# A two-layer kernel: layer 0 put in program order, its gated blocks cut finer, and blocks combined earlier

## The chip, the cores and the metric

One core of one Trainium2 chip runs the whole program in one launch. The metric is device microseconds of that core per execution, as the median of several runs; the profiled execution is a single one. The kernel before has a median of 1210.88 us over 9 runs (1198.3 to 1218.23).

## The reference, cut to what matters

The input x is 16 x 256 tokens of 128 numbers. Each of two layers computes `x + s * silu(g)`, where s comes from a mixing branch and g from a mixture of experts, both of them over the same layer norm of x.

```python
# layer 0
xn = layernorm(x)
q, k, v = xn@Wq, xn@Wk, xn@Wv                 # 4 heads of 128 (q, k) and 32 (v)
gk = log_sigmoid(xn@Wgk1@Wgk2 + bgk2) / 16    # decays
S_t = diag(exp(gk_t)) S_{t-1} + k_t^T v_t     # gated recurrence, per head
o_t = DK**-0.5 * q_t S_t
s = (rmsnorm(o) * gnw * silu(xn@Wg)) @ Wo
comb = top-2 of softmax(xn @ Wg0.T), normed to 1      # 8 experts
h = xn @ W1[e].T + b1[e]; a, b = split(h)
g = sum_e comb[e] * ((a * sigmoid(b)) @ Wo0.T + bo)
x = x + s * silu(g)
# layer 1
xn = layernorm(x)
s = causal_attention(xn, 16 heads of 8) @ w_proj
# top-2 of 16 experts: tanh(xn@mag) * cos(softplus(xn@freq) + 0.1 + phase), times down
x = x + s * silu(rmsnorm(g) * norm_w)
```

## The kernel before, in words

**Tiling.** The 4096 tokens are eight blocks of 512 (`BT`), four tiles of 128 tokens each (`NTL`). A block spans two sequences. All eight blocks stay in SBUF: `xs` holds x, `xns` its norm, `xnTs` the transposed norm; the mixing result `s_sbs[b]` is written over `xnTs[b]`.

**Norms** (`layernorm_T`, L203; `norms`, L653). DVE takes mean and variance (L207, L208), POOL raises to the power -1/2 (L200, L201), DVE scales (L213), PE transposes (L216), ACT copies (L217). Eight matmuls (L448) give a block's scores for the eight experts.

**Routing** (`route`, L237; the same function serves both layers). It picks two experts a token, writes the normed rows with their two weights to DRAM (`xnd`, L276), ranks the tokens by expert and makes lists: `toks` (which rows a tile of 128 slots takes), `rows` (where its results go), `emap` (the expert of each tile). Layer 0 has 71 such tiles, layer 1 has 79. The lists come out of one-hot products on DVE, ACT and PE (L333 to L347) in 16 steps. In all `route` has 25 steps (its yields).

**Gated blocks.** `decays(b)` (L455) computes the decays by ACT (Abs, Exp, Ln, L473 to L475), a running sum by a DVE scan (L478), the two scalings (L485, L488), then q and k scaled by them (L501, L503), `kg`, v and the gate `sg`. Its PSUM tiles of two banks (`pz`, `pq`) come from the pool `p2` with two buffers. `mixed(b)` (L535) multiplies k and q (L544), masks (L545), multiplies by v (L555, L562), norms (L571 to L578) and projects into `s_sbs[b]` (L582). `gated` (L658) interleaves `decays(b)` with `mixed(b - 1)`.

**Layer-0 experts** (`experts0`, L586) go through the 71 tiles in 18 batches of four (the last of three). For a batch POOL fetches the rows by an indirect DMA for each tile (`slot_in`, L368), SP loads the weights of each tile's expert (L601, L603), PE transposes the rows (L608), multiplies (L618), ACT and DVE gate two tiles at a time (L625 to L633), PE multiplies again (L642), DVE adds the bias and weighs (L646, L648), and POOL scatters the results to `yd` (`slot_out`, L380). The fetches of a batch wait for the v copy of a gated block (`vcopies`, with the constants `FIRST` and `SPAN`).

**Order in layer 0.** Norms, routing, experts and gated blocks are emitted interleaved (L670 to L688), and a scheduler of the compiler then places each engine's instructions by its own estimates. Four copies of the layer-1 expert weights from DRAM to DRAM (`late`, L185 to L189, 2 + 2 + 1 + 1 MB) wait for the v copies of the fourth and fifth gated blocks (L689).

**Layer 1** stands under `manual_schedule`: ACT, PE, DVE and SP run in program order, written out by hand. `combined(b)` (L950) loads both results of a block from `yd` (L394; each load waits for every scatter of layer 0), makes the new x, its norm and transpose, and the layer-1 scores. `attention` (L737) yields small pieces, 254 of them with work; `fill(n)` (L1159) emits n pieces and before each of them one POOL instruction, a fetch and a scatter by turns, ordered behind the DVE instruction last marked by `passed`. The combines take `fill(4)` at each of their last eight steps, `route` takes one piece at each of its 25 steps, a batch of eight experts takes about 20, and what is left runs beside `finished(b)`, which ends a block.

Of the kernel before, what the change touches and what calls it, by code (L numbers as in the profile page):

```python
# [10 lines left out]
F32 = mybir.dt.float32  # L11
# [7 lines left out]
P = 128  # L19
# [20 lines left out]
FIRST = 2  # L40
SPAN = 5
PACE = 1
# [18 lines left out]
def two_layer_kernel(  # L61
# [77 lines left out]
    mhalf = cst.tile([P, 16], F32, name="mhalf")  # L139
    nc.gpsimd.memset(mhalf, -0.5)  # L140
# [43 lines left out]
    late = []  # L184
    late.append(nc.sync.dma_start(bank[:, :, 0:H1], freq))  # L185
    late.append(nc.sync.dma_start(bank[:, :, H1 : 2 * H1], mag))
    for c in range(H1 // P):
        cs = slice(2 * H1 + c * D, 2 * H1 + (c + 1) * D)
        late.append(nc.sync.dma_start(bank[:, :, cs], down[:, c * P : (c + 1) * P, :]))  # L189
# [9 lines left out]
    def rsqrt_(out_, var, mul, eps):  # L199
        nc.gpsimd.tensor_scalar(out_, var, mul, eps, ALU.mult, ALU.add)  # L200
        nc.gpsimd.tensor_tensor(out_, out_, mhalf[:, : out_.free_size()], ALU.pow)  # L201

    def layernorm_T(pool, ps, xb, xnT, xn):  # L203
        mv = pool.tile([P, NTL, 2], F32, tag="mv", name="mv")
        for t in range(NTL):
            st = pool.tile([P, 6], F32, tag="st", name="st")
            nc.vector.bn_stats(st, xb[:, t, :])  # L207
            nc.vector.bn_aggr(mv[:, t, :], st)  # L208
        rs = pool.tile([P, NTL], F32, tag="rs", name="rs")
        rsqrt_(rs, mv[:, :, 1], 1.0, 1e-5)  # L210
        pt = ps.tile([P, NTL, P], F32, tag="ps", name="pt")
        for t in range(NTL):
            nc.vector.tensor_scalar(  # L213
                xn[:, t, :], xb[:, t, :], mv[:, t, 0:1], rs[:, t : t + 1], ALU.subtract, ALU.mult
            )
            nc.tensor.transpose(pt[:, t, :], xn[:, t, :], ident)  # L216
        nc.scalar.copy(xnT, pt.rearrange("p t k -> p (t k)"))  # L217
# [19 lines left out]
    def route(pool, ps, sc, ne, slt, lay, emap, rm, tag="ps"):  # L237
# [49 lines left out]
        pc = ps.tile([P, ne], F32, tag=tag, name="pc")  # L287
# [13 lines left out]
        rk = ps.tile([P, ne, NT32], F32, tag=tag, name="rk")  # L301
# [25 lines left out]
        pT = ps.tile([P, 2, slt], F32, tag=tag, name="pT")  # L327
# [60 lines left out]

    def results(pool, lay, b, tag="gg"):
# [35 lines left out]
    nc.gpsimd.dma_start(sb_nw, normw.partition_broadcast(P))  # L425
    with ExitStack() as cg:
        big = cg.enter_context(tc.tile_pool(name="gbig", bufs=2, side="right"))
        wk_ = cg.enter_context(tc.tile_pool(name="gwk", bufs=2, side="right"))
        hp = cg.enter_context(tc.tile_pool(name="ghp", bufs=2, side="right"))
        rt = cg.enter_context(tc.tile_pool(name="grt", bufs=1, side="right"))  # L430
        p2 = cg.enter_context(tc.tile_pool(name="gp2", bufs=2, space=PSUM))
        ps = cg.enter_context(tc.tile_pool(name="gps", bufs=3, space=PSUM))
# [7 lines left out]
        nc.scalar.preload_act_table_set(LN_EXP)  # L440
        held, vcopies = {}, []
        sc0 = rt.tile([P, NT32, E0], F32, name="sc0")
        rm0 = starts(rt, E0)

        def scores(b, w, out_, ne, bias=None):
            pl = ps.tile([P, NTL, ne], F32, tag="ps", name="plg")
            for t in range(NTL):
                nc.tensor.matmul(pl[:, t, :], xnTs[b][:, t * P : (t + 1) * P], w, start=True, stop=True)  # L448
            o = out_[:, b * NTL : (b + 1) * NTL, :]
            if bias is None:  # L450
                nc.scalar.copy(o, pl)
            else:
                nc.vector.tensor_tensor(o, pl, bc(bias.unsqueeze(1), [P, NTL, ne]), ALU.add)

        def decays(b):  # L455
# [6 lines left out]
            nc.scalar.activation(lowT, p_low, AF.Identity, bias=one16)  # L462
            eg = big.tile([P, GH, BT], F32, tag="eg", name="eg", bufs=1)
            eis = []
            mid = wk_.tile([P, GH * NTL], F32, tag="mid", name="mid")
            for u in range(GH // 2):
                hs = slice(2 * u, 2 * u + 2)
# [4 lines left out]
                sp = wk_.tile([P, 2, BT], F32, tag="sp", name="sp", bufs=1)  # L472
                nc.scalar.activation(sp, pz, AF.Abs)  # L473
                nc.scalar.activation(sp, sp, AF.Exp, scale=-1.0)
                nc.scalar.activation(sp, sp, AF.Ln, bias=1.0)  # L475
                nc.vector.scalar_tensor_tensor(sp, pz, 0.0, sp, ALU.min, ALU.subtract)
                cum = wk_.tile([P, 2, BT], F32, tag="cum", name="cum", bufs=1)
# [6 lines left out]
                nc.vector.tensor_tensor(ev, ev, ib(mid[:, 2 * u * NTL : (2 * u + 2) * NTL], CH), ALU.subtract)  # L484
                nc.scalar.activation(eg[:, hs], cum, AF.Exp, scale=1.0 / 16.0)  # L485
                ei = wk_.tile([P, 2, BT], F32, tag="ei", name="ei")
                eis.append(ei)
                nc.scalar.activation(ei, cum, AF.Exp, scale=-1.0 / 16.0)  # L488
                yield
# [3 lines left out]
            for u in range(GH // 2):  # L493
                hs = slice(2 * u, 2 * u + 2)
                for dst_, w_ in ((qg, sb_wq), (kk, sb_wk)):
                    pq = p2.tile([P, 2, BT], F32, tag="p2", name="pq")
                    for c in range(2):
                        h = 2 * u + c
                        nc.tensor.matmul(pq[:, c], w_[:, h * DK : (h + 1) * DK], xnT, start=True, stop=True)
                    if dst_ is qg:  # L500
# [169 lines left out]
        for _ in norms(0):  # L670
            pass
# [590 lines left out]
```

## Time and profile before

| | us |
|---|---|
| median of 9 runs (1198.3 to 1218.23) | 1210.88 |
| the profiled execution | 1219.11 |
| its span, first to last instruction | 1217.4 |
| PE busy | 892.7 (73%) |
| DVE busy | 759.3 (62%) |
| ACT busy | 562.3 (46%) |
| POOL busy | 401.6 (33%) |

PE holds the matmuls, PEld the weight loads that overlap them, DVE the vector engine, ACT the scalar engine, POOL GpSimd, SP the queue that issues most DMAs. The costliest lines of layer 0 on PE are L618 (78.6 us busy), L642 (53.3), L544 (41.4), the two uses of L499 (34.2 and 32.7) and L608 (22.3, with 52.5 us of idle time before it). The mean granted clock of TensorE is 0.847. Sums over the whole span hide that its stages have different limits, so the stages are read one by one.

### The profile page before, as it was taken

What the parts mean: (1) busy time and instruction counts of PE and PEld (TensorE: products, weight loads), DVE (VectorE), ACT (ScalarE), POOL (GpSimd) and SP (SyncE); (2) the same over time, 40 slices, a digit from 0 to 9 for tenths busy, and PEclk for the clock granted to TensorE, in tenths of its full rate; (3) what the DMA queues carried; (4) which work ended last, traced back from release to release, by engine and by line L of the source; (5) the groups of instructions that cost most, each with busy time, mean ns of one, the idle gap of its engine ahead of it and who ended that gap; (6) DMA issues with size and microseconds to landing.
All of it is one profiled execution on the core that took longest, in us unless ns stands there. A gap on an engine that the chain in (4) does not pass through costs nothing. (4 is left out here: it accounts for less than half of the span.)

```text
span 1217.4 us, 17549 instructions
## 1 busy us (share of the span) xinstructions
PE 892.7 (73%) x6394; PEld 628.1 (52%) x6394; DVE 759.3 (62%) x1442; ACT 562.3 (46%) x973; POOL 401.6 (33%) x439
## 2 busy tenths in 40 slices
PE   5858895758798775388656559887888888887762
PEld 3535564545576664244333336565566656665531
DVE  5699673616465522666764636875776688578464
ACT  2335564535466343332211226554555565556283
POOL 4100344323545354001200053472464446343310
PEclk9879897979899887557867769898899899889775
DMA  4060129272333231310040043143134313330231
GB/s 115 1 114 1 35 80 210 76 122 73 87 90 95 77 106 43 91 49 4 13 59 1 0 148 116 34 135 116 43 121 131 124 39 126 122 82 31 68 104 52
DMA packets 88413, 95.40 MB, mean 78 GB/s; under 512 B 22228, under 2 KB 64040, under 8 KB 88328
## 3 DMA queue, kind: packets, MB, share of 16 engines
q1 hardware_dynamic: 78632, 74.32, 22.7%
q0 software_dynamic: 9696, 19.97, 6.4%
q8 instruction: 50, 0.82, 0.3%
q14 instruction: 35, 0.29, 0.1%
HBM read 78.03 MB, written 22.51 MB: 83 GB/s over the span
## 5 line engine op out<-in xcount | busy, mean ns | idle before, releaser
L380 POOL DMA_INDIRECT yd<-og,row x150 | 155.4, 1036 | 265.8 <-DVE og L648 141.0
L832 POOL TENSOR_SCALAR_AFFINE_SELECT pr<-pr 128x1024 f32<-128x1024 f32 x64 | 70.9, 1111 | 318.2 <-ACT pr L829 317.9
L368 POOL DMA_INDIRECT xg<-xnd,tok x150 | 149.1, 994 | 77.5 <-issue 34.7
L822 PE MATMUL Sk<-qm,kT 32*128 32x256 f32 x768 | 129.2, 461 | 42.2 <-ACT pr L829 29.4
L793 PE MATMUL Sq<-km,qT 32*128 32x256 f32 x768 | 132.0, 462 | 11.7 <-DVE negm L803 6.6
L829 ACT ACTIVATE pr<-Sk 128x1024 f32<-128x1024 f32 x96 | 97.4, 1016 | 72.4 <-PE Sk L822 70.9
L803 DVE TENSOR_REDUCE negm<-Sq 128x8 f32<-128x1024 f32 x64 | 78.1, 1220 | 44.6 <-PE Sk L822 26.3
L822 PEld LDWEIGHTS Sk<-qm,kT 32*128 32x128 f32 x768 | 77.1, 216 | 55.4 <-ACT pr L829 37.7
L793 PEld LDWEIGHTS Sq<-km,qT 32*128 32x128 f32 x768 | 73.1, 214 | 61.6 <-issue 37.5
L633 DVE SCALAR_TENSOR_TENSOR gt<-pf,nb,sg 128x128 f32<-128x128 f32 x142 | 40.1, 344 | 81.2 <-ACT sg L629 81.2
L618 PEld LDWEIGHTS pf<-xgT,wt 128*128 128x128 f32 x568 | 73.9, 208 | 12.7 <-issue 6.3
L618 PE MATMUL pf<-xgT,wt 128*128 128x128 f32 x568 | 78.6, 294 | 2.5 <-DVE kk L503 1.3
L625 ACT ACTIVATE sg<-pf,nb 128x128 f32<-128x128 f32 x142 | 40.8, 367 | 59.9 <-PE pf L618 55.3
L642 PE MATMUL pe<-sb_wo,gt 128*128 128x128 f32 x284 | 53.3, 318 | 18.0 <-DVE gt L633 17.5
L642 PEld LDWEIGHTS pe<-sb_wo,gt 128*128 128x128 f32 x284 | 46.3, 221 | 32.4 <-DVE gt L633 22.6
L608 PE MATMUL pxt<-ident,xg 128*128 128x128 f32 x71 | 22.3, 354 | 52.5 <-DMA xg<-xnd,tok 52.4
L1074 PE MATMUL pe<-wt,th 128*128 128x128 f32 x316 | 48.8, 318 | 8.3 <-DVE th L1065 8.3
L787 PE MATMUL Sq<-mq,identb 128*128 128x512 bf16 x128 | 44.1, 430 | 14.7 <-DVE mx L801 7.0
L801 DVE TENSOR_REDUCE mx<-Sq 128x8 f32<-128x1024 f32 x32 | 39.0, 1219 | 24.4 <-PE Sk L822 13.7
L1074 PEld LDWEIGHTS pe<-wt,th 128*128 128x128 f32 x316 | 45.2, 228 | 15.7 <-issue 10.1
L1026 ACT ACTIVATE z<-pf 128x512 f32<-128x512 f32 (+1 forms) x40 | 23.7, 593 | 52.3 <-PE pf L1022 52.3
L1034 DVE SCALAR_TENSOR_TENSOR vt<-z,wt 128x256 f32<-128x256 f32 x79 | 45.8, 620 | 1.4
(278 smaller groups left out, 2046.3 us busy)
## 6 DMA issues: line engine op xcount, KB each, us to landing
wt<-bank SPq DMA_DIRECT2D x79, 385.0 KB
wt<-in_w_dram SPq DMA_DIRECT2D x71, 256.0 KB
gg<-yd SPq DMA_DIRECT2D x32, 256.0 KB
xnd<-xnx SPq DMA_DIRECT2D x16, 260.0 KB
xg<-xnd,tok POOLq DMA_INDIRECT x150, 2.9
yd<-og,row POOLq DMA_INDIRECT x150, 3.9
x<-in_x_dram SPq DMA_DIRECT2D x8, 256.0 KB
bank<-in_freq_dram SPq DMA_DIRECT2D x1, 2048.0 KB
```

The costliest lines, as they stand in the source:

```text
L368: return nc.gpsimd.indirect_dma_start(out=xg[:, i, :], out_offset=None, in_=xnds[lay], in_offset=bass.IndirectOffsetOnAxis(ap=toks[lay][:, ...
L380: give = nc.gpsimd.indirect_dma_start(out=yds[lay], out_offset=bass.IndirectOffsetOnAxis(ap=rows[lay][:, j : j + 1], axis=0), in_=og[:, i, ...
L618: nc.tensor.matmul(pf[:, i, c, :], wts[i0 + i][:, c * P : (c + 1) * P], xgT[:, i0 + i, :], start=True, stop=True,)
L642: last = nc.tensor.matmul(pe[:, i, :], gts[i // 2][:, i % 2, c, :], sb_wo0[:, c, :], start=(c == 0), stop=(c == 1))
L787: nc.tensor.matmul(S[:, c], identb, mq, start=True, stop=False, skip_group_check=True)
L793: nc.tensor.matmul(S[:, c, js, :], qT[part][r, tq], km[r, js, tk], start=not diag, stop=True, skip_group_check=True,)
L803: passed(nc.vector.tensor_reduce(ng, S, AX.X, ALU.max, negate=True))
L822: nc.tensor.matmul(S[:, c, js, :], kT[part][r, tk], qm[r, js, :], start=True, stop=True, skip_group_check=True,)
L829: nc.scalar.activation(pr, S, AF.Exp, scale=scale)
L832: pooled(nc.gpsimd.affine_select(pr_, pr_, pattern=[[0, 8], [1, P]], compare_op=ALU.is_ge, fill=0.0, base=0, channel_multiplier=-1,))
L1034: nc.vector.scalar_tensor_tensor(v[:, ks, :], z[:, ks, :], INV2PI, ib(wts[i0 + i][:, WROW - 2 :], P), ALU.mult, ALU.add)
L1074: nc.tensor.matmul(pe[:, i - i0, :], ths[i // 2][:, 2 * (i % 2) + c, :], wts[i][:, 2 * H1 + c * D : 2 * H1 + (c + 1) * D], start=(c == 0), ...
```

## The change

Layer 0 now also stands under `manual_schedule`: ACT, PE, DVE and SP follow the program's text, with this driver in place of the interleaving at L670 to L690:

```diff
         main = gated()
-        for _ in main:
...
+        with tc.manual_schedule(engines={ET.Activation, ET.PE, ET.DVE, ET.SP}):
+            nc.scalar.preload_act_table_set(LN_EXP)
+            with tc.tile_pool(name="gpn", bufs=2, space=PSUM) as pn, tc.tile_pool(name="grt", bufs=1, side="left") as rt:
...
+                for _ in normed0(0, pn):
+                    pass
+                copies = bank_copies()
+                first = itertools.chain(
+                    staged(normed0(b, pn) for b in range(1, NB)),
+                    route(rt, pn, sc0, E0, SLT0, 0, emap0, rm0, "n", {"tag": "nT", "bufs": 1}),
+                )
+                for i, _ in enumerate(first):
+                    if i % 2:
+                        next(main)
+                    if i >= 12:
+                        next(copies, None)
...
+            due = 0.0
+            for _ in experts0(hp, pe_):
+                spread()
+                due += 1.0 / RATE
+                while due >= 1.0:
+                    due -= 1.0
+                    next(main, None)
...
+            with tc.tile_pool(name="gpc", bufs=2, space=PSUM) as pc_:
+                c_ps[:] = [pc_, "pc"]
+                cstream = staged([combined(b) for b in range(NB)], lambda b: b in mixed_)
+                for _ in main:
+                    next(cstream, None)
```

`bank_copies` yields the four DRAM copies one after the other, on SP's queue, without a wait. `staged` (moved up from layer 1) starts one generator a step and advances all that have started. `RATE` is 0.85. Counted from the text: the norms take 10 steps and route 25, with 17 gated pieces beside them; the experts take 109 steps with 128 pieces; 31 pieces are left for the last loop, and at its start six blocks are mixed.

**Norms.** `normed_T` serves both layers; ACT takes Ln and Exp where POOL took a power:

```diff
-        rsqrt_(rs, mv[:, :, 1], 1.0, 1e-5)
+        nc.scalar.activation(rs, mv[:, :, 1], AF.Ln, bias=eps5)
+        nc.scalar.activation(rs, rs, AF.Exp, scale=-0.5)
+        yield
```

**Gated blocks.** `decays` has ten pieces and `mixed` twelve (seven and four before). The parts of `decays` become functions and are emitted like this; the arithmetic is the same:

```diff
-        p2 = cg.enter_context(tc.tile_pool(name="gp2", bufs=2, space=PSUM))
-        ps = cg.enter_context(tc.tile_pool(name="gps", bufs=3, space=PSUM))
+        p2 = cg.enter_context(tc.tile_pool(name="gp2", bufs=1, space=PSUM))
+        ps = cg.enter_context(tc.tile_pool(name="gps", bufs=2, space=PSUM))
...
+            logs(0)
+            yield
+            sums(0)
+            logs(1)
+            yield
+            scales(0)
+            yield
+            sums(1)
+            scaled(0, qg, sb_wq)
+            yield
+            scales(1)
+            scaled(0, kk, sb_wk)
+            yield
+            scaled(1, qg, sb_wq)
+            yield
+            scaled(1, kk, sb_wk)
+            yield
```

`logs` holds the pz matmuls and the three ACT instructions, `sums` the DVE instructions up to the subtraction (L476 to L484), `scales` the two Exp, `scaled` a pq and its DVE instruction. The tiles `sp` and `cum` get a second buffer.

**Experts.** They have PSUM of their own (`pf` two banks, one bank `pe` for the transposes and the second product), go tile by tile, and ask for the rows and weights of the next batch at the start of a batch. `wanted` and `given` are the lists of fetches and scatters still to be issued:

```diff
+            for k, (j0, n) in enumerate(batches):
+                xg, wts, nbs = got
+                if k + 1 < len(batches):
+                    got = loads(*batches[k + 1])
+                gts, pend = [], []
+                for i in range(n):
+                    pf = pe_.tile([P, 4, P], F32, tag="pf", name="pf0", bufs=2)
...
+                    for f in pend:
+                        f()
...
+                    pend = [gate]
+                    gts.append(gt)
+                    yield
+                for f in pend:
+                    f()
+                if k + 1 < len(batches):
+                    while any(args[1] == 0 for args in wanted):
+                        fetch(1)
+                    xgT = turned(got[0], batches[k + 1][1])
+                yield
+                pe = pe_.tile([P, CP0, D], F32, tag="pe", name="pe0", bufs=1)
...
+                given.extend((og, 0, j0 + i, i) for i in range(n))
+                yield
+            give(len(given))
```

`gate` of a tile (the two DVE instructions of L633) is emitted one step late. `turned` holds the transposes and the xgT copy. `loads` puts a batch's rows on `wanted` and issues its weight loads on SP (six weight buffers, five before; three row buffers, two before).

**The POOL queue.** `fetch`, `give`, `behind`, `pooled` and `passed` are moved from layer 1 to where both layers reach them; the body of `fill`'s turn-taking becomes

```diff
+    def spread():
+
+        turn[:] = [not turn[0]]
+        if wanted and (turn[0] or not given):
+            fetch(1)
+        else:
+            give(1)
```

Each fetch and scatter waits for the DVE instruction marked last (`behind`), and keeps the program's order on POOL (`pooled`). In layer 0 one `spread` goes with each of the experts' steps: six for a batch of four. Many DVE instructions of `decays`, `mixed` and the experts are now marked.

**Combines.** `combined` moves to layer 0 with its text as it was (its tiles get two buffers throughout, `gg` among them); what is left of it after the last gated piece runs with three attention pieces a step:

```diff
-                for i, _ in enumerate(staged([combined(b) for b in range(NB)])):
-                    if i >= 4:
-                        fill(4)
...
+            for _ in cstream:
+                fill(3)
```

By count the first seven blocks are combined in the loop over the last gated pieces, and four steps are left for the eighth. Route 1 and the layer-1 experts take their attention pieces as before, 25 and 169; layer 1 else differs only in the side of SBUF on which some pools lie.

## The prediction

> **What bounds the kernel now.** I read the stages first: busy time of each engine in stretches cut where the trace shows a stage begin or end (columns: stretch, then PE, PEld, DVE, ACT, POOL busy us with instructions, granted clock, DMA share, GB/s).
>
> ```profile
> 13.40:66.60 53.20, 41.39 (x132) 26.03 (x132) 36.06 (x110) 18.93 (x33) 9.64 (x13) 0.88 0.11 25
> 66.60:121.60 55.00, 40.44 (x257) 27.13 (x258) 51.78 (x87) 26.96 (x37) 1.50 (x8) 0.84 0.39 64
> 121.60:160.00 38.40, 33.08 (x227) 21.95 (x226) 25.62 (x53) 24.86 (x39) 10.17 (x12) 0.91 0.17 42
> 160.00:300.00 140.00, 101.99 (x668) 74.47 (x668) 69.13 (x119) 71.40 (x139) 51.03 (x48) 0.89 0.51 114
> 300.00:440.00 140.00, 117.88 (x791) 89.57 (x790) 74.72 (x139) 75.78 (x151) 66.10 (x64) 0.90 0.33 92
> 440.00:487.00 47.00, 27.00 (x158) 24.02 (x156) 12.46 (x36) 14.93 (x38) 21.28 (x24) 0.79 0.24 62
> 487.00:590.00 103.00, 70.27 (x380) 42.93 (x380) 69.42 (x173) 33.92 (x61) 6.24 (x6) 0.67 0.15 43
> 590.00:703.00 113.00, 58.76 (x396) 33.98 (x394) 71.57 (x112) 20.60 (x26) 12.90 (x18) 0.73 0.13 22
> 703.00:1145.00 442.00, 369.82 (x3185) 268.10 (x3185) 305.60 (x511) 234.02 (x334) 207.25 (x203) 0.92 0.30 95
> 1145.00:1217.40 72.40, 32.03 (x210) 19.88 (x210) 39.34 (x89) 39.62 (x117) 5.78 (x5) 0.65 0.31 87
> ```
>
> PE is the engine that lasts in nearly every stretch. The first 121.6 us hold the norms, route 0 and the first gated pieces; 121.6 to 487 are the layer-0 experts, the last 47 us of it with no gated work left beside them; 487 to 590 are the eight combines with 32 attention pieces; then route 1, the layer-1 experts and the tail. Layer 1 is already in program order and keeps PE 84% busy (369.8 of 442). In 121.6 to 487 PE is busy 280 of 365.4 us. What it waits for there, up to 440, the list of waits says (total us, times, longest):
>
> ```profile
> DVE gt L633 <- ACT sg L629: 66.0, 18, 13.8
> PE pxt L608 <- DMA xg<-xnd,tok: 42.2, 22, 7.6
> PE pe L642 <- DVE gt L633: 13.0, 12, 2.1
> ```
>
> The first is DVE's idle time and costs nothing. PE's own large wait is the second: the transposes of fetched rows, 2.9 us a batch over the page's 18 batches (52.4). So the price of a fetch matters; the timeline shows one (start, us, engine, line):
>
> ```profile
> 460.55 0.69 DVE L648 TENSOR_TENSOR og<-og,xg 128x512 f32<-128x512 f32 x1
> ...
> 461.52 1.01 POOL L380 DMA_INDIRECT yd<-og,row  x1 [7.60 <-DVE og L648]
> ...
> 466.66 0.99 POOL L368 DMA_INDIRECT xg<-xnd,tok  x1 [0.30 <-issue]
> ...
> 467.95 0.96 POOL L368 DMA_INDIRECT xg<-xnd,tok  x1 [0.30 <-issue]
> ...
> 470.18 0.45 PE L608 MATMUL pxt<-ident,xg 128*128 128x128 f32 x1 [4.70 <-DMA xg<-xnd,tok]
> ...
> 471.61 0.48 PE L608 MATMUL pxt<-ident,xg 128*128 128x128 f32 x1 [0.56 <-DMA xg<-xnd,tok]
> ```
>
> DVE ends at 461.24 and POOL starts 0.28 later; POOL takes 1.28 us a fetch; the transpose runs 3.5 to 3.7 us after its fetch began, and 3.2 to 3.6 in the batch before that (452.84 to 456.05). I use 3.3.
>
> **The change, stage by stage.** The trace of before is the clock of this sum: its span is 1217.4, the profiled run 1219.1, which is 0.7% over the median of 1210.9.
>
> *Norms and route 0.* POOL's rsqrt (0.43 and 1.01 us a block, and it started at 9.2 behind POOL's setup) becomes two ACT instructions (0.30 and 0.20 by L969, L970), so block 0 no longer waits for POOL until 13 us. Seven norms need 2.8 us of DVE each (bn 4 x (0.28 + 0.17), xnx 4 x 0.34), five gated pieces beside them 8 us: some 40 us from 4.5, so route 0 starts near 44; before, the last scores left PE at 57. Route 0 has 25 steps and 12 gated pieces beside them. Its own DVE work I put at 35 us (ohp 9.7, ohj 12, the rest by its lines' layer-0 share); a gated piece has 0.91 us of DVE (160 us over the rows L476 to L578, 176 pieces). 46 us at the 94% of the stretch 66.6 to 121.6 is 49, plus 4 for the ACT step inside each chunk: the stage ends at 97 (85 to 110), with 17 pieces done, where before ended at 121.6 with about 38 (five scans, seven mask copies).
>
> The four bank copies (6 MB) move from 186 and 250 to route 0, behind the xnd stores on SP's queue. They held DMA at 0.51 over 160 to 300, where PE idles 38 us against 22 in 300 to 440; that loss goes, but they may still run when the first experts load. I charge 10 us (6 to 18) for the start: four fetches (4 x 1.28 + 3.3) with little beside them, and the rest of the copies.
>
> *Experts with 128 gated pieces.* PE's work: 280 us in before's stretch, which holds the 18 batches and some 138 pieces; a piece is 1.16 us (PE's rows L460 to L582 sum to 219; cut by the tenth by which all layer-0 rows together exceed the union of 362, and over 176). So 280 - 10 x 1.16 = 268. On top come PE's waits:
>
> (a) The fetch. A batch has four steps with one POOL instruction each between its start and the next batch's transposes, and gives and fetches take turns: two rows are fetched, and two are left (none in batch 0, one in batch 16). Those are issued in one go, behind the last gate of this batch, and the transposes follow at once in PE's program order. From the end of the fourth tile's matmuls: 0.2 to ACT, 0.57 for two Exp, 0.9 for Ln and Exp at 128x256 (timeline at 480), 0.3 in hand-overs, 0.57 for the gate on DVE: 2.4. Then 0.28 + 1.28 + 3.3 and a last transpose of 0.45: 7.7. In it PE has 1.18 gated pieces (1.4) and the other transposes (about 1.3, in the gaps). So 5.0 idle, 16 times: 80 us (4.3 to 6 each: 69 to 96). POOL, ACT and DVE queue behind the same wait, since the xgT copy and everything after it depends on it.
>
> (b) One buffer in place of two under pz and pq (4 banks to 2). pz of the second half waits for Abs, Exp, Ln (3.1) and the DVE op (1.22) of the first, 4.7 with hand-overs, against 3.4 of PE work between (one mixed piece, 1.7 expert steps of 1.3): 1.3. The scan's piece holds DVE 4.4 us (1.22 + 2.28 + 0.17 + 0.69), while tile gates and mask copies stand behind it: 2 us twice a block. With 0.7 for the rest, 6 us a block, 5.8 blocks, a quarter absorbed by (a): 26. No row shows this order; the bounds are 10 (DVE and ACT are under half busy) and 50 (idle share of layer 1's in-order stretch, 16.3%, on top of (a)).
>
> 268 + 80 + 26 + 10 = 384, so this stage ends at 481 (345 to 420 long), 6 us before its old end, but with 31 gated pieces still to do.
>
> *31 pieces and seven combines.* The first combine waits as before: og's end at 484.0 to acc at 492.9 there, 9 us, of which two pieces cover 2. Combining is 6.1 us of DVE a block (four 128x512 ops, four bn pairs, four xnx, sc: L954 to L983). Six blocks come in ten steps beside ten pieces: 37 + 9 = 46 us of DVE, in one queue. The last 21 pieces run with no experts beside them: block 6's pair and block 7's twelve alone, which took 431 to 443 there with the scheduler's order; I put 28. Sum 7 + 46 + 28 = 81 (65 to 95), to 562. The eighth combine is some 11 us of chain under 12 attention pieces: 22 us, to 584. Before stood at 590 then, but with 32 pieces of attention done; now 12.
>
> *The rest.* Route 1 and the layer-1 experts are unchanged step for step (25 and 169 pieces): 113 + 442, to 1139. The attention left for the tail grows from 28 pieces to 47. In the tail 28 pieces took 1145 to 1190, 1.6 us each, so 19 more are 30 (15 if the output steps, now nearer PE's 44% than its limit, hide half): 72.4 + 30, to **1241**. That is 24 over before: 1210.9 + 24 = **1235**.
>
> The Trainium skill speaks against the change at one place. The page "TensorE: Matmul & The Clock Gate", section "HAM oscillation — how this bites in real kernels", says that an idle gap of more than about 3.4 us drops PE to half clock; by it 16 gaps of 5 us could cost 16 x 1.7 = 27 us more, a span of 1268. The rows here: clock 0.89 at 73% busy (160 to 300, xg waits included), 0.79 at 57% (440 to 487). The experts would be 70% busy (268 of 384), so I keep the durations as measured at 0.89 and charge nothing.
>
> **Rivals.** *Tight order* (0.27, faster). Fine pieces fill the gaps, and the experts run at layer 1's 84%: 268/0.837 + 10 = 330, 54 less: span 1187, time 1181. For it: layer 1 does this with the same helpers. Against: there 20 fetch-or-give slots serve 16 rows a batch, here 6 serve 8. It decides if PE's idle in the stage falls under 92 us, 5.1 a batch, where I have 6.4.
>
> *DVE's queue* (0.13, slower still). Where (b) is 50 and the combines' 46 us of DVE stretch to 60, waiting for PE in turn: +38, time 1273. For it: DVE 94% busy in 66.6 to 121.6; against: 49 and 53% in the two long stretches of the experts, and 48% by this sum (183 of 384).
>
> *Paid back* (0.12, about no change). The tail absorbs half its pieces (-15) and the start costs 6: time 1216; then the change only moves work.
>
> **The numbers.** Forecast 0.48, its own range 1210 to 1262. Bounds of the terms, added as independent (12, 38, 15, 15), give 45 either way; with the tight order below and the DVE queue above I give 1180 to 1275. What one measurement tells from no change is 0.5%, 6 us. Faster: 0.27 and a quarter of "paid back", 0.30. Same: the rest of it and 0.02, 0.11. Slower: 0.59.
>
> **What would show it.** Right: PE waits for xg at the batch's transposes, 70 us or more in total, in pairs behind the gate; fewer than 20 attention pieces before route 1; the last exponential of attention about 30 us nearer the end of a longer tail. Wrong: layer-0 experts ended before 450; the transposes' wait under 40 us; or PE's wait moved to pz and pq.

## The result and the profile after

The changed kernel takes 1351.07 us (median of 20 runs, 1346.72 to 1358.48) against 1212.07 for the kernel before (62 runs, 1198.3 to 1222.87): a ratio of 1.1176, 95% interval 1.1151 to 1.1201. It is slower, as forecast, but by 139 us where 24 were forecast, and 1351 lies far above the range of 1180 to 1275. The profiled execution has a span of 1344.8; the sum of the prediction was 1241.

The same cut into stages as before, for the changed kernel (stretch, length, PE, PEld, DVE, ACT, POOL busy us with instructions, granted clock, DMA share, GB/s):

```profile
46.00:111.00 65.00, 31.33 (x150) 18.44 (x150) 50.39 (x90) 20.29 (x27) 1.72 (x8) 0.66 0.84 130
111.00:549.00 438.00, 299.61 (x1736) 224.25 (x1737) 179.33 (x318) 201.30 (x426) 142.33 (x140) 0.79 0.24 65
549.00:650.00 101.00, 57.10 (x315) 41.28 (x313) 61.25 (x147) 39.24 (x69) 3.63 (x6) 0.66 0.15 44
650.00:678.00 28.00, 21.59 (x109) 11.31 (x110) 18.52 (x49) 4.92 (x11) 1.89 (x4) 0.75 0.00 1
678.00:792.00 114.00, 56.42 (x356) 32.34 (x356) 70.24 (x104) 18.98 (x24) 13.98 (x18) 0.69 0.14 26
792.00:1232.00 440.00, 368.81 (x3173) 266.24 (x3174) 304.81 (x513) 236.18 (x337) 207.09 (x201) 0.92 0.30 94
1232.00:1344.80 112.80, 65.91 (x448) 39.15 (x447) 55.64 (x114) 48.53 (x126) 12.08 (x11) 0.69 0.20 56
```

The cuts are: the end of route 0 (111), the last weighing of layer-0 results (549), the seventh combine's scores (650), the eighth's (678), the lists of route 1 (792), the last scatter of layer 1 (1232). Beside the forecast:

| stage | before | forecast | after | over forecast |
|---|---|---|---|---|
| route 0 ends at | 121.6 | 97 | 111 | +14 |
| layer-0 experts | 365 | 384 | 438 | +54 |
| 31 gated pieces and seven combines | – | 81 | 101 | +20 |
| eighth combine, 12 attention pieces | 103 (eight combines, 32 pieces) | 22 | 28 | +6 |
| route 1 | 113 | 113 | 114 | +1 |
| layer-1 experts | 442 | 442 | 440 | -2 |
| tail | 72 | 102 | 113 | +10 |

Against before, the experts stage gave 73 us more, the 31 pieces with the combines 26 more, the tail 40 more, and route 0 gave 11 back. In the experts stage the waits of PE from 112 to 549 show two things (total us, times, longest):

```profile
PE pxt L695 <- DMA xg<-xnd,tok: 100.1, 51, 6.9
PE pz L510 <- DVE sp L519: 12.3, 4, 3.7
PE pq L546 <- DVE sp L519: 10.5, 5, 3.3
PE p_s L650 <- DVE yT L646: 6.0, 4, 2.0
```

The transposes now wait 100 us for fetched rows, against 52 before, in 51 waits: four in the first batch (9.8 us), one in the second, and 46 in the sixteen after, nearly three a batch. Idle time in the stage is 138 us (438 - 299.6), of which this wait is 100. The other thing stands in the first list: PE's *busy* time, 299.6 us where the forecast had 268. The timeline of one batch shows both at once (start, us, engine, line):

```profile
295.88 0.98 POOL L377 DMA_INDIRECT xg<-xnd,tok  x1 [0.35 <-DVE gt L729]
...
296.21 0.27 PE L695 MATMUL pxt<-ident,xg 128*128 128x128 f32 x1
...
298.93 0.48 PE L695 MATMUL pxt<-ident,xg 128*128 128x128 f32 x1 [2.45 <-DMA xg<-xnd,tok]
299.52 0.60 DVE L729 SCALAR_TENSOR_TENSOR gt<-pf,nb,sg 128x128 f32<-128x128 f32 x2
300.39 0.96 POOL L377 DMA_INDIRECT xg<-xnd,tok  x1 [3.53 <-DVE gt L729]
301.65 0.94 POOL L377 DMA_INDIRECT xg<-xnd,tok  x1 [0.30 <-issue]
302.96 0.48 PE L695 MATMUL pxt<-ident,xg 128*128 128x128 f32 x1 [3.56 <-DMA xg<-xnd,tok]
304.20 0.48 PE L695 MATMUL pxt<-ident,xg 128*128 128x128 f32 x1 [0.76 <-DMA xg<-xnd,tok]
...
306.18 3.33 PE L746 MATMUL pe<-sb_wo,gt 128*128 128x128 f32 x16
```

The last gate ends at 300.12; 0.27 later POOL starts the third row's fetch, 1.26 later the fourth's; each transpose runs some 2.6 us after its fetch began. That is the chain the forecast described. Not in it: the second row is late too (2.45 at 298.93; its fetch, one issued by turns, began only at 295.88). And each of these transposes takes 0.48 us, where the first of the batch took 0.27 (at 296.21); the sixteen output matmuls behind the gaps take 3.33 us, where the same sixteen take 1.95 in a kernel without the gaps (e15, shown with its run).

The granted clock says why. Its records change at multiples of 3.41 us, so the same stretch is cut into slices of that length (the granted clock is the third number from the end):

```profile
292.01:295.42 3.41, 2.44 (x22) 2.27 (x21) 2.34 (x6) 2.79 (x8) 1.85 (x2) 1.00 0.54 122
295.42:298.83 3.41, 1.06 (x4) 0.26 (x3) 0.19 (x1) 3.19 (x8) 1.09 (x2) 1.00 0.56 152
298.83:302.24 3.41, 0.48 (x1) 0.18 (x1) 1.21 (x3) 0.04 (x1) 1.55 (x2) 0.50 0.08 16
302.24:305.66 3.42, 1.94 (x4) 1.10 (x5) 0.00 (x0) 0.59 (x1) 1.35 (x2) 0.50 0.15 42
305.66:309.07 3.41, 3.41 (x15) 2.89 (x15) 0.00 (x0) 1.32 (x2) 0.00 (x0) 0.50 0.00 0
309.07:312.49 3.42, 1.39 (x13) 1.20 (x12) 2.87 (x6) 1.46 (x4) 1.00 (x1) 1.00 0.25 73
```

PE is busy for 1.06 us of the slice that ends at 298.83, and from there the clock is 0.50; it is 1.00 again behind a slice in which PE is busy throughout. In the whole stage it falls to 0.50 23 times, each time behind a slice with PE busy for 10 to 49% of it. So the idle time right before an instruction doesn't settle how long that takes: in the next batch of this trace a transpose takes 0.33 us after 2.55 us of idle time, because the clock is still 1.00 there (it falls at 326.14):

```profile
324.49 0.33 PE L695 MATMUL pxt<-ident,xg 128*128 128x128 f32 x1 [2.55 <-DMA xg<-xnd,tok]
```

Where the gated pieces run beside the combines, one more wait shows, at the first combine:

```profile
557.75 0.69 DVE L759 TENSOR_TENSOR acc<-gg 128x512 f32<-128x512 f32 x1 [7.47 <-DMA gg<-yd]
...
561.11 2.08 PE L510 MATMUL pz<-lowT,sb_wgk 32*128 32x512 f32 x4 [11.60 <-DVE sp L519]
```

DVE stands for 7.5 us at the first combine's add, waiting for results that have to be scattered to DRAM and loaded back. The DVE instruction that would free the buffer of pz (L519) is behind it in DVE's queue, so PE idles 11.6 us, with gated work of its own that doesn't need the combine.

### The profile page after: what moved, and what is told of

It reads as the page before. It is cut to its first block, busy times and chain, and to the rows that moved or that the text cites. A ratio compares the mean times of both kernels' runs of the same rounds, so it can differ in the third digit from the quotient of the medians.

```text
span 1344.8 us, 17744 instructions
## 1 busy us (share of the span) xinstructions
PE 931.2 (69%) x6394; PEld 653.7 (49%) x6394; DVE 770.7 (57%) x1442; ACT 589.2 (44%) x1059; POOL 390.7 (29%) x422
## 5 line engine op out<-in xcount | busy, mean ns | idle before, releaser
L389 POOL DMA_INDIRECT yd<-og,row x150 | 151.6, 1011 | 274.9 <-DVE og L750 135.6
L377 POOL DMA_INDIRECT xg<-xnd,tok x150 | 152.2, 1015 | 217.4 <-DVE gt L729 75.3
L695 PE MATMUL pxt<-ident,xg 128*128 128x128 f32 x71 | 28.2, 408 | 100.1 <-DMA xg<-xnd,tok 100.1
L718 ACT ACTIVATE sg<-pf,nb 128x128 f32<-128x128 f32 x142 | 44.1, 361 | 67.1 <-PE pf L713 66.1
L695 PEld LDWEIGHTS pxt<-ident,xg 128*128 128x128 f32 x71 | 11.9, 170 | 119.7 <-DMA xg<-xnd,tok 108.4
L729 DVE SCALAR_TENSOR_TENSOR gt<-pf,nb,sg 128x128 f32<-128x128 f32 x142 | 42.9, 344 | 43.6 <-ACT sg L722 39.6
L748 DVE TENSOR_TENSOR og<-pe,sb_bo 128x512 f32<-128x512 f32 (+1 forms) x18 | 12.3, 685 | 80.1 <-PE pe L746 80.1
L746 PEld LDWEIGHTS pe<-sb_wo,gt 128*128 128x128 f32 x284 | 52.1, 280 | 10.5 <-issue 6.1
L697 ACT COPY xgT<-pxt 128x512 f32<-128x512 f32 (+1 forms) x18 | 10.4, 580 | 102.4 <-PE pxt L695 102.4
L346 ACT ACTIVATE ohj<-ohj,place 128x568 bf16<-128x568 bf16 (+1 forms) x16 | 12.7, 795 | 94.5 <-DVE ohj L345 94.5
L351 PE MATMUL pT<-ohj,ohp 128*128 128x142 bf16 (+1 forms) x128 | 17.0, 305 | 53.3 <-DVE ohj L349 53.3
```

The lines of the kernel that those rows point to most:

```text
L377: return nc.gpsimd.indirect_dma_start(out=xg[:, i, :], out_offset=None, in_=xnds[lay], in_offset=bass.IndirectOffsetOnAxis(ap=toks[lay][:, ...
L389: give = nc.gpsimd.indirect_dma_start(out=yds[lay], out_offset=bass.IndirectOffsetOnAxis(ap=rows[lay][:, j : j + 1], axis=0), in_=og[:, i, ...
L718: nc.scalar.activation(sg[:, c, :], pf[:, 2 + c, :], AF.Exp, scale=-1.0, bias=nbs[i][:, 2 + c : 3 + c])
L729: passed(nc.vector.scalar_tensor_tensor(gt[:, c, :], pf[:, c, :], nbs[i][:, c : c + 1], sg[:, c, :], ALU.add, ALU.mult))
L746: nc.tensor.matmul(pe[:, i, :], gts[i][:, c, :], sb_wo0[:, c, :], start=(c == 0), stop=(c == 1))
```

## The experiments

The runs were spread over several chips. On some the kernel before takes about 1210 us and the changed one has a ratio of 1.118; on others before takes about 1260 and the changed one 1.084 (c_after) or 1.090 (e17). Ratios are therefore compared within a set, or with a control on the same kind of chip: the first, second and fifth set ran on the slower kind, the third and fourth on the faster. The theory: the two fetches left to the end of a batch, and the clock that falls behind them, are the main loss. Rivals: the one buffer under pz and pq; the combines beside the gated pieces; the bank copies.

### First set: one edit each (before 1261.93)

**e1_early** issues all fetches of the next batch when its loads are emitted:

```diff
                     got = loads(*batches[k + 1])
+                    fetch(len(wanted))
```

> All rows of the next batch are fetched at the start of a batch, so nothing is left to fetch behind the last gate. Theory A (the wait for the two late fetches of a batch, and the half clock that follows each such gap of PE): PE's wait for xg falls from 100 us to under 20, PE busy falls from 931 to 890-905 because the clock rises from 0.80 to 0.84 or more, and the time falls by 100 to 130 us, to 1220-1250. Rival B (the machine is short of other things: one buffer under pz and pq, chains through ACT and DVE): the idle time comes back at pz, pq and the gates, and the time stays above 1300.

1316.3 us, ratio 1.0452 (1.0363 to 1.0542), which is 0.039 under the control of the second set, 49 us. The wait for rows falls to 10.1 us, the stage from 437 (in that control) to 388, its PE work to 280.2. New in its place: 24.1 us at the output matmuls for ACT's copy of the transposes, and 42.9 in place of 27.3 at pz. Half of what the theory asked for came; the idle time that came back at pz and a time above 1300 are what rival B said. The stage of the control, then of e1:

```profile
113.00:550.00 437.00, 297.21 (x1731) 222.58 (x1731) 178.68 (x317) 200.88 (x425) 142.63 (x139) 0.79 0.23 65
112.80:500.50 387.70, 280.23 (x1735) 213.80 (x1736) 178.94 (x320) 199.52 (x426) 143.38 (x139) 0.83 0.26 73
```

**e2_latecomb** runs the combines in layer 1 again, beside attention:

```diff
                 for _ in main:
-                    next(cstream, None)
+                    pass
...
-            for _ in cstream:
-                fill(3)
+            for i, _ in enumerate(cstream):
+                if i >= 4:
+                    fill(4)
```

> The combines go back to layer 1, behind the last gated piece, with four attention pieces a step from the fifth step on; the gated pieces stay as they are. If combining beside the last gated pieces is a loss (DVE's queue holds the gated pieces back: 101 us for that stretch where 81 were forecast), the time falls by 10 us or more; if it is a gain, the time rises by 20 to 40 us. Theory A, that the fetches do it, says nothing on it but leaves at most 30 us for it.

1330.3 us, ratio 1.0571 (1.048 to 1.0662), 0.027 under the control of the second set: combining beside the last gated pieces is a loss. The 31 pieces alone take 55.5 us, the eight combines with 32 attention pieces 68, together 123.5 against 129 when they were mixed; the tail is 75 against 113.

**e3_order** issues the second half's Abs, Exp and Ln after the first half's q and k, so that pz finds its buffer free:

```diff
             logs(0)
             yield
             sums(0)
-            logs(1)
...
+            scales(0)
+            yield
+            scaled(0, qg, sb_wq)
+            yield
+            scaled(0, kk, sb_wk)
+            yield
+            logs(1)
```

> The pieces of a block's decays are put in another order: the second half's pz comes only after both uses of the first half's pq, so that pz and pq, which share one buffer, follow each other at two pieces' distance where ACT and DVE lie between. Rival B: PE's waits for the sp instruction at pz and pq (46 us) all but go, and the time falls by 45 to 70 us. Theory A: these waits fall, but part of it comes back at the transposes; 15 to 35 us.

1392.73 us, ratio 1.1068 (1.0977 to 1.1158). The waits at pz and pq for the earlier user of the buffer fall to 3 us, and the wait for rows grows to 122.9; the stage takes 457. A miss, some 0.02 over the control of the second set: the wait at pz only gave way to a longer one for rows.

**e4_latecopies** puts the four bank copies at four late expert steps in place of route 0 (`if i in (24, 25, 42, 43): next(copies)`).

> The four copies of the expert weights leave route 0 and are issued at steps 24, 25, 42 and 43 of the experts. If they slow route 0 and the first batches (stage ended at 111 where 97 was forecast, DMA at 0.84), the experts start about 10 us earlier and the time falls by 5 to 15 us; if route 0 has its length from its own chain, the start stays at 111 and the fetches beside the copies get slower: 0 to 20 us more.

1378.5 us, ratio 1.0965 (1.0866 to 1.1063). Route 0 ends at 110.8, as before; the first batch takes 30.0 us against 30.2. The copies cost nothing where the change put them; later they go with a wait for rows of 115.8 in place of 101, and a ratio 0.012 over the control of the second set.

### Second set: combinations, with a control (before 1260.09)

> The changed kernel once more, on the chip of this set, as the bar for the three others: 1.118 times the kernel before if chips keep the ratio; up to 1.13 if the price of a fetch differs between chips (its wait for xg is then over 110 us where the first profile had 100).

The changed kernel: 1368.31 us, ratio 1.0842 (1.0777 to 1.0907), span 1367.5. Neither figure expected: the ratio isn't the same on the two kinds of chip, and the wait for rows is 101.

> Early fetch and combines put back, together. If the two losses are separate (theory A for the fetch; the attention pieces lost beside the combines for the other), they add: 90 to 115 us under the changed kernel, 1.02 to 1.04 times the kernel before. If they are one loss seen twice, the pair gains no more than the larger of the two, 60 to 75 us.

e5 has the edits of e1 and e2: 1279.99 us, ratio 1.0149 (1.0091 to 1.0207), 88 under the control. The two losses add, as the theory said: 0.039 and 0.027 apart, 0.069 together.

> The new order of a block's pieces, on top of the last one. Alone it gained next to nothing, because PE's waits at pz and pq (gone: 46 to 2 us) came back at the transposes (100 to 123). Theory A says that with the fetch early there is nothing left where they could come back: 20 to 35 us under the last one. Rival: the chain of a block's ACT and DVE work sets the pace and the order is worth nothing here either, within 8 us.

e6 adds the order of e3: 1314.95 us, ratio 1.0432 (1.0349 to 1.0516), a miss: 35 over e5. PE's wait at the output matmuls for the copy of the transposes grows from 22.6 to 57.8.

> On top of the last one, the transposes take their PSUM from the two pf banks and no longer share one bank with the second product. In the early-fetch kernel PE waits 24 us for the xgT copy there. If that wait counts: 12 to 24 us under the last one, and about level with the kernel before or a little under it (0.98 to 1.00). If it only moves to pf: within 5 us.

e7 adds to e6 a bank pair for the transposes:

```diff
-                pt = pe_.tile([P, CP0, P], F32, tag="pe", name="pxt0", bufs=1)
+                pt = pe_.tile([P, CP0, P], F32, tag="pf", name="pxt0", bufs=2)
```

1278.23 us, ratio 1.0123 (1.0065 to 1.0182). That wait is gone. In the new order the bank pair is worth 37 us, more than either figure expected; order and bank pair together gain nothing over e5.

### Third set: how much gated work beside what (before 1208.13)

> Rows fetched right after the loads, combines back in layer 1, and the transposes of fetched rows in the bank pair of the gates (tag pf) in place of the output matmuls' bank; the gated pieces in the order of the change. Theory (PE's program order, bank by bank): the 22.6 us that PE waited at the output matmuls for the copy of the transposes go, and nothing takes their place: layer-0 experts 387 -> 365 to 372, wait for pz about 30, ratio to before 0.995 to 1.003 (1.015 without the bank pair). Rival (one bank was only where the wait showed; the copy stands in ACT's queue behind the Abs, Exp, Ln of the gated pieces): the wait moves to the next matmul that reads the copy, stage 380 or more, ratio 1.01 or over.

e8 is e5 with the bank pair, in the order of the change: **1189.38 us, ratio 0.984 (0.9769 to 0.9911)**, under both kernels and better than the theory asked (0.995 to 1.003, a stage of 365 to 372). Its stages from the end of route 0 on:

```profile
112.70:435.00 322.30, 259.75 (x1732) 200.45 (x1733) 179.07 (x320) 199.04 (x426) 145.00 (x139) 0.90 0.31 88
435.00:491.00 56.00, 38.05 (x262) 25.08 (x262) 44.04 (x101) 31.01 (x53) 4.51 (x7) 0.86 0.24 70
491.00:556.00 65.00, 52.84 (x294) 31.98 (x295) 46.13 (x114) 19.42 (x33) 5.64 (x7) 0.78 0.03 9
```

The experts take 322 us in place of 438, with as many PE instructions (1732 and 1736 in the records) and 40 us less of PE's time on them. The eight combines with 32 attention pieces take 65 (before: 103).

> As the first, with 0.68 in place of 0.85 expert steps to a gated piece, so that all 159 gated pieces lie beside the layer-0 experts and none after. Theory (with the fetch ahead PE's idle of some 95 us in the stage is room): the 56 us in which 31 gated pieces ran alone go, the stage grows by 20 to 35, since 31 x 1.16 = 36 us of PE's work is partly absorbed: ratio 0.97 to 0.985. Rival (the stage is bound by the one buffer under pz and pq and each gated piece brings its own wait): the stage grows by 50 or more, ratio as without it, 0.995 or over.

e9 has `RATE = 0.68`: 1210.56 us, ratio 1.0004 (0.9976 to 1.0031). The rival's figure, though not quite by its cause: the stage grows by 42 us for 31 pieces, which is less than the 56 they took alone, but the combines then take 97 in place of 65, since nothing covers the way of the last results through DRAM.

> As the second, with no gated pieces beside the norms and route 0, and 0.61 steps to a piece, so that all 176 lie beside the experts. This measures the term 'norms and route 0 end at 97', which was 111. Theory (DVE's own queue sets that stage, and a gated piece's 0.91 us of DVE delays it): route 0 ends near 95, 16 us earlier; the 17 pieces cost 15 to 20 in the experts: time within 6 us of the second's. Rival (the chain between DVE, PE and ACT in route 0 sets it and the pieces only fill its gaps): route 0 ends at 106 or later, and the time is 10 to 20 longer than the second's.

e10: 1221.96 us, ratio 1.011 (1.0075 to 1.0145). Its first stage:

```profile
0.00:87.40 87.40, 36.67 (x168) 28.71 (x168) 60.32 (x178) 18.52 (x44) 9.52 (x44) 1.00 0.69 130
```

Without gated pieces norms and route 0 end at 87.4, 25 us earlier than in e8, which is 1.5 us for each of the 17 pieces. The theory was right on that. But the 17 pieces cost 37 in the experts (401 against 364) where 15 to 20 was expected, so the time is 11 us worse: the rival's figure, without its reason.

> As the second, with the second half's Abs, Exp, Ln issued after the first half's q and k matmuls (so that pz of the second half finds its buffer free). With the bank pair this was worth -2 us in the run before, an 11 us shorter expert stage against 6 us in the gated pieces that ran alone. Theory (the wait for pz is what is left of the one-buffer term): with no pieces alone only the gain remains, 5 to 11 us under the second. Rival (the wait for pz only changes its place): within 5 us of the second, or longer.

e11: 1228.46 us, ratio 1.0168 (1.0101 to 1.0236), 18 over e9. The rival holds: the order is a loss here too.

### Fourth set: the parts, one at a time (before 1212.87)

> The changed kernel with one edit alone: the transposes of fetched rows use the bank pair of the gates (tag pf) in place of the bank of the output matmuls. Theory (with the late fetch in place the wait for the copy is hidden behind it: pe<-xgT shows 1.9 us there): ratio to before 1.10 to 1.125, wait for xg 90 to 100 as before. Rival (the shared bank is a main cause by itself): ratio 1.09 or less, experts stage 30 us or more shorter than 438.

e12 is the change with the bank pair alone: 1344.52 us, ratio 1.1096 (1.1035 to 1.1156). Some 9 us under the change's 1.1176, within what both intervals leave, and as the theory said: no main cause.

> Early fetch and late combines with the shared bank, measured before at 1.015 where the kernel before took 1260, again beside the kernel with the bank pair's tag, which was 0.984 where before took 1208. Theory (the bank costs some 30 us once the fetch is early, since the output matmuls wait for ACT's copy of the transposes and the clock falls in those gaps): 1.01 to 1.03, pe<-xgT about 20 us, PE's busy time in the stage 15 to 20 us over 260. Rival (the difference was the chip's): 0.98 to 0.99.

e13 is e5 on the other kind of chip: 1203.81 us, ratio 0.992 (0.9886 to 0.9953). Between the figures of theory and rival, and nearer the rival's: of the way from 1.015 to 0.984 most was the chip's. The rest, 0.8%, is the bank pair's at most, since the two intervals overlap; the stage is 337 against 322, PE's work 268.4 against 259.8, the wait for the copy 11.6.

> Early fetch, late combines, bank pair, and 0.76 expert steps to a gated piece: 143 pieces beside the experts and 16 after (128 and 31 at 0.85, ratio 0.984; 159 and none at 0.68, ratio 1.000). Theory (a piece costs 1.3 us beside the experts and 1.8 alone, and the pieces alone cover the wait for the first combine's gathered rows, some 20 us at the first combine when there are none): 15 pieces moved gain 7, the other 16 are 28 us, enough to cover it: ratio 0.976 to 0.982. Rival (the cost in the experts and the lost cover are even along the way, a straight line between 0.984 and 1.000): 0.99 to 0.995.

e14: 1192.16 us, ratio 0.9834 (0.9779 to 0.989), the same as e8. Both figures missed: what the 15 moved pieces gain (342 + 27 against 322 + 56), the combines give back (76 against 65).

> Early fetch and bank pair, with the combines beside the last 31 gated pieces as in the change. Against 0.984 with the combines in layer 1. Theory (combining beside the gated pieces stretches both and takes 20 attention pieces' cover away, which come back in the tail): 1.01 to 1.025, the tail 105 to 115 us against 77. Rival (combining beside costs only where the clock was low): 0.98 to 0.995.

e15 differs from e12 by the early fetch alone, and from e8 by the place of the combines alone: 1233.38 us, ratio 1.0202 (1.015 to 1.0253), as the theory said, the tail too. So with the bank pair, on this kind of chip, the late fetch is worth 0.089 of the time before, 108 us, and the combines beside gated pieces 0.036, 44 us. The experts stage in e12 and then the costliest groups that changed (busy us, mean ns of one, idle before):

```profile
113.40:549.50 436.10, 298.31 (x1735) 224.23 (x1735) 179.71 (x320) 200.94 (x426) 142.25 (x139) 0.80 0.23 65
```

```profile
L746 PE MATMUL pe<-sb_wo,gt 128*128 128x128 f32 x284 | 53.0, 366 | 0.0
L695 PE MATMUL pxt<-ident,xg 128*128 128x128 f32 x71 | 27.9, 405 | 100.1 <-DMA xg<-xnd,tok 94.5 <-DVE gt L729 3.4 <-ACT sg L721 2.1
```

and the same of e15, with the stretch behind the experts (its tail is 113.8 us, e8's 77):

```profile
110.70:432.80 322.10, 257.73 (x1734) 197.21 (x1735) 179.25 (x320) 199.37 (x426) 144.64 (x139) 0.90 0.31 88
432.80:534.60 101.80, 57.38 (x317) 41.54 (x315) 61.66 (x152) 39.88 (x70) 4.16 (x7) 0.66 0.15 44
```

```profile
L747 PE MATMUL pe<-sb_wo,gt 128*128 128x128 f32 x284 | 37.5, 287 | 0.8 <-DVE gt L730 0.8
L695 PE MATMUL pxt<-ident,xg 128*128 128x128 f32 x71 | 15.1, 319 | 17.9 <-DMA xg<-xnd,tok 13.6 <-ACT sg L723 2.0 <-DVE gt L730 1.4
```

and from its timeline the sixteen output matmuls of the batch shown above:

```profile
307.91 1.95 PE L747 MATMUL pe<-sb_wo,gt 128*128 128x128 f32 x16
```

The same 284 output matmuls take 53.0 us and 37.5, the same 71 transposes 27.9 and 15.1. One edit, which moves no PE work, takes 114 us from the stage: 73 of idle time and 41 of busy time. The clock column says the same, 0.80 and 0.90: by the clock's records e12 spent 177 of its 436 us at 0.50 and e15 61 of its 322, the rest at 1.00.

### Fifth set: the gap by itself (before 1258.42)

The early fetch removes the wait and the gap together. e16 keeps the wait and fills the gap, with work that is thrown away:

```diff
                 for i in range(n):
+                    for _ in range((0, 6, 10, 3)[i]):
+                        nc.tensor.transpose(pt[:, i, :], ident, ident)
                     nc.tensor.transpose(pt[:, i, :], xg[:, i, 0:D], ident)
```

> The changed kernel with the late fetch left as it is, and 6, 10 and 3 extra transposes of a constant ahead of the second, third and fourth transpose of each batch, into the same place of the same bank, overwritten by the real ones: 339 of them, 92 us of PE at 0.27 us each, put where PE waits for the rows. They take no wait away; they only keep PE busy in it. It measures the step 'I keep the durations as measured at 0.89 and charge nothing'. Theory (the idle gap itself lowers the clock of the matmuls behind it): transposes of rows, now 28.2 us, under 20; output matmuls, now 52.6 us, 38 to 45; expert stage 438 -> 395 to 415, time 20 to 45 under the changed kernel's. Rival (the clock follows the work of a longer stretch, or the gap sets nothing): the rows' durations stay as they are and the time is the same to 30 longer.

> The changed kernel itself, beside the former on the same chip: the same as before, ratio 1.11 to 1.12 where the kernel before takes about 1210, 1.08 to 1.09 where it takes about 1260.

e16: 1356.84 us, ratio 1.0815 (1.0735 to 1.0895); the control 1366.86, 1.0898 (1.0813 to 1.0984). The whole times can't be told apart by these intervals; the stage can be read. e16 first, then its extra transposes (L696), the output matmuls and the transposes of rows; the control's stage last:

```profile
111.90:532.20 420.30, 320.40 (x2074) 251.50 (x2075) 179.63 (x320) 200.96 (x426) 142.27 (x139) 0.87 0.25 67
```

```profile
L696 PE MATMUL pxt<-ident 128*128 128x128 f32 x339 | 56.7, 316 | 0.0
L748 PE MATMUL pe<-sb_wo,gt 128*128 128x128 f32 x284 | 43.8, 319 | 1.9 <-ACT xgT L699 1.9
...
L697 PE MATMUL pxt<-ident,xg 128*128 128x128 f32 x71 | 25.7, 361 | 59.7 <-DMA xg<-xnd,tok 59.1
```

```profile
113.10:549.40 436.30, 295.87 (x1734) 221.36 (x1735) 179.54 (x320) 201.00 (x426) 142.27 (x139) 0.80 0.24 65
```

With 339 instructions *more* on PE the stage is 16 us shorter. Without the extra ones PE's work is 263.7 us (320.4 - 56.7) against 295.9. That is 32 us less, but the extra transposes overlap the real ones in the records, and PE's other instructions by themselves cover 275.8; so between 20 and 32 us of the control's PE time is the slower clock behind the gaps. The clock is at 0.50 for 109 us of e16's stage and for 171 of the control's. The output matmuls came out as the theory said (43.8, in 38 to 45), the transposes of rows not (25.7, where under 20 was expected: the gap still lies in part ahead of them), and the stage is 16 shorter where 23 to 43 were expected, since the extra work (56.7) and the rest of the wait (59.1) together take 15 us more than the control's wait did (100.8).

## Why the prediction was wrong

**Right in kind.** The side (slower), the place and the mechanism of the largest loss: PE waits 100.1 us for rows at the transposes (70 or more was named), behind the last gate, with POOL, ACT and DVE behind it; 12 attention pieces before route 1 (fewer than 20 was named); the tail 113 us where it was 72. Its last exponential, though, came only 6 us nearer the end than before (26 us ahead of it in place of 32), where 30 was named. The one-buffer term (b) was forecast at 26 and measured 23 (12.3 + 10.5 + 0.6 at pz and pq). Route 1 and the layer-1 experts came out within 2 us. *Tight order*, *paid back* and *DVE's queue* all fell; e8 shows what the first would have needed, the early fetch.

**The step that failed: "so I keep the durations as measured at 0.89 and charge nothing".** PE's work of 268 us became 299.6, the largest single term of the 54 us in the stage. e16 put the clock's part at 20 to 32 us by filling the gaps, e12 against e15 at 41 by removing them. The mistake was to read the clock from the mean busy share of long stretches. PE was forecast 70% busy and came out at 68%, yet the clock was 0.79 and not 0.89: the idle time sat in one lump at the same place of each batch, and the instructions that paid were those behind it. The prediction's own first table had a row against the step: 487 to 590, with PE busy 68% (70.27 of 103.00) and a clock of 0.67. The Trainium skill was set aside there with a reason. Its page "TensorE: Matmul & The Clock Gate", section "HAM oscillation — how this bites in real kernels", describes a loop whose every round waits for a DMA and starts the next at half clock; by it the prediction had 27 us, at 1.7 a gap. The page counts half of its 1.67 us as lost, so by its loop 16 gaps would be an estimate of 13. The runs say 20 to 41. The trace agrees on the half clock (0.50 from 298.83 on), but not on the length of the gap: the clock fell there at the end of 2.35 us without PE work, under the 3.4 of the page.

**Terms that were mis-sized.** (a), 80: measured 90 beside the first batch's 10, since nearly three rows a batch are late and not two; the forecast counted the two left over but took the one fetched last by turns to be there. (Its parts from the last matmuls to the gate also add up to 2.5 us and not 2.4.) The rest of the idle time, 15 us at p_s, pf and pe, had no term (-3 for (b), +10, +15 and +32 make the 54). Norms and route 0, 97: measured 111; a gated piece beside them costs 1.5 us (e10 against e8) where its DVE time of 0.91 was charged, 10 of the 14. Pieces with combines, 81: measured 101; a gated piece alone costs 1.8 us (55.5 for 31 in e2) where 28 for 21 was put, and the first combine holds PE 11.6 us where 7 was put. The tail's 30: measured 40, 1.8 us a piece (37 for 20, e15 against e8) where 1.6 was put.

What the errors share: a piece of work was priced at its busy time, or at its price in a stretch full of other work, and used where it ran with less beside it.

**The combines.** The forecast let them cost and save about the same: 81 and 22 against 103 before. The runs add that moving them gains nothing by itself (118.9 us in e15 against 56 + 65 in e8) and costs 37 in the tail, because twenty attention pieces lose the combines as cover.

**What stays open.** Why before and after differ by 4% and 1% between the two kinds of chip wasn't tried. The stages say where: the changed kernel is longer in the layer-1 experts (461 us in c_after, 440 in the first profile), the kernel of e5 and e13 there (464 and 442) and in the layer-0 experts (387 and 337). So what the early fetch is worth depends on the chip too, and its 49 us (e1) and 108 (e15) differ by the bank pair and by the chip, which weren't told apart. Whether the kernel before would gain from the late combines' cover alone wasn't either. e8's 19 us under the kernel before were read stage by stage (experts 322 against 365, combines 65 against 103, and 56 of pieces alone that before doesn't have), not taken apart by an experiment.

## What to carry to other kernels

In an order written by hand, count which DMAs are issued only at their deadline: taking turns on a slow queue left nearly three rows of four late, and one line that issues them a batch ahead was worth 108 us of 1345 on one kind of chip, with the bank pair, and 49 us of 1368 by itself on the other. Price an idle lump on PE twice, once as waiting and once as slower matmuls behind it; a mean busy share doesn't show the second. And before covered work is moved, name what it was covering: here the attention pieces that came back in the tail.

## What was unexpected of the hardware

- Adding 339 transposes to PE's waits shortened the stage from 436.3 to 420.3 us.
- In the changed kernel's layer-0 experts the clock fell to 0.50 23 times, behind slices of 3.41 us in which PE was busy for 10 to 49%; the whole slice need not be idle. Transposes of rows took 0.27 or 0.33 us at 1.00 and 0.42 to 0.48 at 0.50; output matmuls 366 ns in the mean in e12 and 287 in e15.
- Chips differ: the kernel before takes 1208 to 1213 us in some sets and 1258 to 1262 in others, and one kernel (e5, e13) is slower than it by 1.5% on the one and faster by 0.8% on the other.
- In the batch shown, an indirect fetch of 128 rows held POOL 1.26 us until the next started, and the rows were used 2.6 to 3.1 us after it began (300.39 to 302.96, 295.88 to 298.93), where the prediction took 3.3 from the trace before.
